# Attention over sixteen images on one core: second-pair block sums made on VectorE instead of stored and loaded, sums in fixed places, old weight form for a fourth image

## Chip, cores and metric

The kernel runs on one core of a Trainium2 chip. The metric is device time in microseconds for one launch, as the median of several runs. A second number, the time of one profiled execution, belongs to the trace that is read here.

## What is computed

The reference is a self-attention block over x of shape (16, 512, 32, 32), in float32:

```
xn = group_norm(x, 8 groups) * gamma + beta          # per image, over 64 channels x 1024 positions
q, k, v = split(qkv_w (1536 x 512) @ xn + qkv_b)     # 1x1 convolution, 4 heads of 128 channels
attn = softmax(q^T k / sqrt(128))                    # per head, 1024 x 1024
out = x + proj_w (512 x 512) @ (attn v) + proj_b
```

So each image has four heads, each with two products of 1024 x 1024 x 128, and four projections of 512 x 512 x 1024.

## The kernel before

**The main loop.** It runs over 16 images, 4 heads and 8 steps of 128 keys. A step has two halves; in each, TensorE makes a tile of scores (L1580, 128 x 512), ScalarE its exponential (L1586), and TensorE the weighted sum of the step before (L1677). VectorE adds up the exponentials for the denominators (L1601). Between these, each half-step gets a few *units* of projection work, taken from the list `halfway`. A unit is one product of a Strassen scheme, with the loads, sums and results that belong to it. Each engine's instructions stand in an order that comes from this emission and from priorities (`tc.high_priority` puts the steps that free an accumulator ahead).

**Two forms of the projections.** Images 0 to `OLD - 1` use the old form: q and k of a pair of heads, or v of all, are seven products of blocks, each again seven products, in four groups (`two_levels`, matmuls at L742, 256 columns wide). The output projection of every image has this form too. From image `OLD` on, `thirds` makes q, k and v together from x cut in three along the positions (`S3`, 342 wide): 15 products for each pair of heads, each again seven products (`strassen`, matmuls at L1168, 171 wide). These 15 are taken in eight groups (`THIRDS`) of one or two, so an image has 16 groups G: 0 to 7 for the first pair of heads, 8 to 15 for the second. A group is seven units, and a new group starts every four units. The 112 units lie in head 2 and head 3 of the image before and in head 0 of the image itself. The table `OUTER`/`FACTORS` names the seven products; the order within a group is `ORDER = (1, 2, 6, 5, 7, 4, 3)`.

**What a group needs.** First, *forms*: sums and differences of blocks of x (`FORMS_B`, made on VectorE by `make_forms`, L1043, 11 of them in six groups). Second, four inner sums t1 to t4 of the forms (`make_sum`, L1089 and L1092). Third, weights, stored earlier in DRAM as sums too (`load_weights`, on SP's queue, L1108). Both pairs of heads need the same forms and inner sums. Before, they are made for the first pair, stored to DRAM by POOL's queue (L1046 and L1095), and loaded back for the second pair by SP's queue (`load_forms` L1054, `load_sum` L1099). `HOMES` says in which of three sets of buffers a group's four sums lie, and `FOLLOWS` after which group each second-pair group may be loaded. In the function `before(k)` of `group_units`, these steps are put ahead of the k-th unit of a group: weights for the next group at k = 0 and 3, forms of the next at 1, sums of the next at 2 to 5, loads of later sums at 3 to 6, and forms to be loaded for the group after next at 3.

**Results of a group.** `out_` (L1192) adds an accumulator and an earlier copy on VectorE and so frees the accumulator; `combine` (L1256, L1265, L1278) builds q, k and v from them; `turn_v` (L982) transposes v in blocks and sends it through DRAM.

**The builder.** The weights' forms for `thirds` are made on the chip during the old-form images: `form_steps` (L1394 load, L1413 adds, L1420 stores, laid out by `BUILD_A` as head, tiles, half-steps) and then `inner_steps` for each group of the first pair (L1449 to L1452, laid out by `BUILD_B`). For the second pair, the first new-form image itself loads weights at L1429 and L1441 through `load_quads`, sums them in `sum_weights` (L1449 on) and stores them for the images after it.

Of the kernel before, what the change touches and what calls it, by code (L numbers as in the profile page):

```python
# [16 lines left out]
P = 128  # L17
# [97 lines left out]
def attention_block(  # L115
# [63 lines left out]
KC = 2  # L179
# [33 lines left out]
BUILD_B = (  # L213
    ((4, "v", (3, 10)), (5, None, (1, 8))),
    ((6, "o", (1, 8)),),
    ((8, "v", (3, 10)),),
)
FOLLOWS = {
    5: (8,), 7: (9,), 8: (10,), 9: (11,), 10: (12,), 11: (13,), 12: (14, 15),
}  # L220
# [6 lines left out]
def fast_path(ctx, tc, x, sources, out, consts, flag, dims):  # L227
# [140 lines left out]
    def halves(tiles, prefix):  # L368

        b = {  # L370
            f"b{r + 1}{h + 1}": [tiles[2 * r + k][:, ts(h, HALF)] for k in range(KC)]
            for r in range(2) for h in range(2)
        }
        b["t1"] = b["b12"]
        for n in ("t2", "t3", "t4"):
            if prefix == "x":
                t = tpool.tile([P, KC, HALF], F32, tag="f", bufs=3, name=f"x{n}")
                b[n] = [t[:, k] for k in range(KC)]
                continue
            b[n] = [  # L380
                tpool.tile([P, HALF], F32, tag=f"{prefix}{n}{k}", name=f"{prefix}{n}{k}")
                for k in range(KC)
            ]
        return b
# [269 lines left out]
    def two_levels(name, site, b, blocks, finish, sums="make", homes="BBBB", prepare=None):  # L654
# [17 lines left out]

        def sum_tile(g, m):
            k = int(m[1]) - 1
            tag = f"in_{m}" if homes[g] == "B" else f"ot{2 + k // 2}{k % 2}"
            if homes[g] == "C":
                if k % 2 == 0:
                    pairs[g] = ppool.tile([P, N], F32, tag="p", name=f"{name}_{g}_{m}")
                t = pairs[g][:, ts(k % 2, HALF)]
            else:  # L680
                t = tpool.tile([P, HALF], F32, tag=tag, name=f"{name}_{g}_{m}")
            haves[g][m] = t.rearrange("p (i q) -> p i q", q=Q)
            return haves[g][m][:, : len(OUTER[g])]

# [320 lines left out]
    def thirds(b):  # L1005
# [23 lines left out]

        def make_forms(G):  # L1030
            p, g = parts(G)
            if p or g not in FORMS_B:
                return
            n = size(G)
            forms[G] = tpool.tile([P, KC, 2, W3], F32, tag="f", bufs=3, name=f"f_{b}_{G}")

            def of(what):
                return wide_x(b, *what) if isinstance(what, tuple) else made[what]

            for i, (f, op, a, c) in enumerate(FORMS_B[g]):  # L1040
                made[f] = forms[G][:, :, i, :]
                eng = nc.vector
                (eng.tensor_add if op == "+" else eng.tensor_sub)(made[f], of(a), of(c))  # L1043
            t = dpool.tile([P, KC, n, W3], F32, tag=f"f_{g}", bufs=1, name=f"keptf_{b}_{g}")
            inner_kept[b, g, "f"] = t
            nc.gpsimd.dma_start(t, forms[G][:, :, :n, :])  # L1046

        def load_forms(G):
            p, g = parts(G)
            if p == 0 or g not in FORMS_B:  # L1050
                return
            n = size(G)
            forms[G] = tpool.tile([P, KC, 2, W3], F32, tag="f", bufs=3, name=f"f_{b}_{G}")
            nc.sync.dma_start(forms[G][:, :, :n, :], inner_kept[b, g, "f"])  # L1054

        def sum_tile(G, m):
            k = int(m[1]) - 1
            n = size(G)
            home = HOMES[G]
            tag = {"A": f"ot{2 + k // 2}{k % 2}", "B": f"in_{m}", "C": f"sg_{m}"}[home]  # L1060
            t = tpool.tile(
                [P, H3 if home == "C" else HALF], F32, tag=tag, name=f"s_{b}_{G}_{m}"
            )
            sums[G, m] = t[:, : n * H3].rearrange("p (i q) -> p i q", q=H3)
            return sums[G, m]

        def make_sum(G, m):
            p, g = parts(G)
            if p:
                return  # L1070
            n = size(G)
            to = sum_tile(G, m)
            a, c = {
                "t1": ("b12", "b11"), "t2": ("b22", "t1"), "t3": ("t2", "b11"),
                "t4": ("b21", "t2"),
            }[m]
# [16 lines left out]
            t = dpool.tile([P, n, H3], F32, tag=f"{m}_{g}_", bufs=1, name=f"kept3_{m}_{g}")  # L1093
            inner_kept[b, g, m] = t
            nc.gpsimd.dma_start(t, to)  # L1095

        def load_sum(G, m):
            g = G % count
            nc.sync.dma_start(sum_tile(G, m), inner_kept[b, g, m])  # L1099

        def load_weights(G, t):
            p, g = parts(G)
            m, n = PARTS[t], size(G)
            wts[G, t] = wpool.tile([P, 2, m, P], F32, tag=f"w{t}", name=f"w{t}_{b}_{G}")
            if first and p:
                load_quads(p, g, t, wts[G, t], nc.sync)
            else:
                nc.sync.dma_start(wts[G, t][:, :n], store3[p, g, t])  # L1108

        def sum_weights(G):  # L1110
            p, g = parts(G)
            if first and p:
# [43 lines left out]
        def group_units(G):  # L1156
# [192 lines left out]
        sizes = (2, 2) + (2, 3, 2) * 15 + (1, 2)  # L1349
        assert sum(sizes) == len(units)  # L1350
        halves_ = []
        for n in sizes:
            halves_.append(units[:n])
# [1 line left out]
        return halves_  # L1355

    store3, builder = {}, {}
    negq = one.tile([P, HEADS], F32, name="negq")
    for p_ in range(PAIRS):
        for g_, group_ in enumerate(THIRDS):  # L1360
# [116 lines left out]
    def lay_builder():  # L1477
# [9 lines left out]
        for head, where, firsts, last in BUILD_A:  # L1487
            if where:
                at(head, firsts[0], lambda where=where: take(where))
            for first in firsts:  # L1490
                for i, step in zip((0, 2, 3, 5, 6), form_steps(*chunks.pop(0))):
                    at(head, first + i, step)
            if last:
                at(head, 15, builder.clear)
        assert not chunks
        groups = [(0, g) for g in range(len(THIRDS))]
        turn = 0
        for run_ in BUILD_B:
            first = True
# [886 lines left out]
```

## Time and profile before

| | |
|---|---|
| median of 3 runs | 3219.69 us (3209.53 to 3223.44) |
| profiled execution | 3236.49 us |
| its span, first to last instruction | 3234.8 us |
| mean granted TensorE clock in it | 0.995 |

The span is that of one execution with the profiler on, 1.7 us shorter than the time of the same execution. Sums below are made against 3236.5 us and then set against the median. In the trace, x_y names with their numbers left out stand for the tiles: f is a form of x, s_t an inner sum, w weights, t_x and t_y the two accumulators, r the results, keptf and kept_t the copies in DRAM, a_o and a_v the builder's tiles.

### The profile page before, as it was taken

To read this page: it belongs to the slowest core of one execution; us is meant where nothing else is said; L and a number is where in the kernel's file an instruction comes from. 1 tells how busy PE (TensorE), PEld (TensorE's weight loads), DVE (VectorE), ACT (ScalarE), POOL (GpSimd) and SP (SyncE) were. 2 spreads that over 40 slices of the span, in tenths; PEclk is the share of its full clock that TensorE was granted. 3 is DMA by queue.
4 is the path that set the end of the run, shared out by engine and by line. 5 is a ranking of instruction groups with operands and counts; after the bars stand their busy time and mean duration, and the time that the engine had idled before them with its cause. 6 is when DMAs were issued, how large, how long until landed. Compare 5 with 4: busy or idle time off the path is not lost.

```text
span 3234.8 us, 40108 instructions
## 1 busy us (share of the span) xinstructions
PE 3143.8 (97%) x12056; PEld 2271.2 (70%) x12056; DVE 2758.0 (85%) x4959; ACT 1565.7 (48%) x3288; POOL 676.6 (21%) x1225
## 2 busy tenths in 40 slices
PE   9999999999999999999999999999999999999999
PEld 7556667677767777677777677777777767777775
DVE  9989989789698897978969789798897978979797
ACT  3534435355454554545445454454544545545443
POOL 0122122213022130321303213032131221312110
PEclk9999999999999999999999999999999999999999
DMA  5576766978869687796877967779687786877961
GB/s 172 180 233 217 250 192 197 267 244 228 253 213 280 214 240 245 224 281 207 243 234 224 273 208 235 242 225 289 207 245 248 234 265 196 262 240 236 285 194 48
DMA packets 310572, 741.67 MB, mean 229 GB/s; under 512 B 44528, under 2 KB 143616, under 8 KB 310352
## 3 DMA queue, kind: packets, MB, share of 16 engines
q1 hardware_dynamic: 200512, 410.48, 41.8%
q0 software_dynamic: 88528, 285.31, 27.6%
q10 hardware_dynamic: 21312, 43.26, 4.7%
q8 instruction: 99, 1.62, 0.2%
q14 instruction: 121, 0.99, 0.1%
HBM read 515.53 MB, written 223.35 MB: 228 GB/s over the span
## 4 chain that ended last, share of the span: by engine, by line
PE 53%; DVE 18%; DMA 12%; issue 4%; ACT 1%; POOL 1%; SPq 0%; ACTq 0%; DVEq 0%; POOLq 0%
PE s L1580 15%; PE po L1677 15%; PE t_x L1168 9%; PE t_y L1168 7%; DMA w<-kept 6%; PE pp_x L742 4%; PE pp_y L742 3%; DVE tot L1601 3%; DMA s_t<-kept_t 3%; DVE vu L982 2%; DVE r L1192 2%; DMA row<-r 1%; DVE r L1256 1%; DVE s_t L1089 1%; DVE y L1552 1%
## 5 line engine op out<-in xcount | busy, mean ns | idle before, releaser
L1580 PE MATMUL s<-qk,qk 128*128 128x512 f32 x2048 | 1051.3, 595 | 0.2 <-ACT p L1586 0.2
L1677 PE MATMUL po<-p,v 128*128 128x512 f32 x2048 | 1051.1, 595 | 0.0
L1586 ACT ACTIVATE p<-s 128x512 f32<-128x512 f32 x1024 | 610.5, 596 | 777.7 <-PE s L1580 741.6
L1677 PEld LDWEIGHTS po<-p,v 128*128 128x128 f32 x2048 | 615.8, 301 | 375.8 <-issue 258.6
L1601 DVE TENSOR_TENSOR tot<-tot,p 128x1024 f32<-128x1024 f32 (+1 forms) x408 | 471.6, 1156 | 130.2 <-ACT p L1586 128.8
L1168 PEld LDWEIGHTS t_x<-s_t,w 128*128 128x128 f32 x2340 | 397.0, 191 | 227.9 <-issue 150.0
L1168 PE MATMUL t_x<-s_t,w 128*128 128x171 f32 x2340 | 444.8, 309 | 0.8 <-DMA w<-kept 0.8
L1580 PEld LDWEIGHTS s<-qk,qk 128*128 128x128 f32 x2048 | 361.8, 190 | 37.2 <-issue 12.9
L1095 POOL DMA_DIRECT2D kept_t<-s_t x416 | 224.1, 541 | 341.8 <-DVE s_t L1089 222.7
L990 POOL DMA_DIRECT2D vd<-vu x120 | 65.8, 548 | 1089.0 <-DVE vu L982 1082.9
L1256 DVE TENSOR_TENSOR r<-r,r 128x684 f32<-128x684 f32 x286 | 243.1, 865 | 6.4 <-issue 0.2
L1192 DVE TENSOR_TENSOR r<-t_y,t_u 128x342 f32<-128x342 f32 (+1 forms) x416 | 201.3, 484 | 41.3 <-ACT t_u L1127 31.5
L1168 PE MATMUL t_y<-f,w 128*128 128x171 f32 x1144 | 203.3, 310 | 21.7 <-DVE r L1192 21.6
L1168 PEld LDWEIGHTS t_y<-f,w 128*128 128x128 f32 x1144 | 175.3, 190 | 27.7 <-DVE r L1192 27.7
L1192 DVE TENSOR_TENSOR r<-t_y,t_p 128x342 f32<-128x342 f32 x208 | 101.1, 486 | 108.1 <-ACT r L1131 94.2
L1127 ACT COPY t_u<-t_x 128x342 f32<-128x342 f32 x260 | 108.4, 417 | 167.6 <-PE t_x L1168 150.4
L742 PE MATMUL pp_x<-pp_t,w_proj 128*128 128x256 f32 x630 | 167.1, 382 | 8.2 <-ACT pp_u L613 8.2
L742 PEld LDWEIGHTS pp_x<-pp_t,w_proj 128*128 128x128 f32 x630 | 117.5, 190 | 77.2 <-issue 32.5
L1556 POOL DMA_DIRECT2D out_y<-y x120 | 65.6, 547 | 467.7 <-DVE y L1555 425.9
L995 POOL DMA_DIRECT2D v<-vd x240 | 139.6, 589 | 98.5 <-DMA vd<-vu 79.4
L1168 PE MATMUL t_y<-s_t,w 128*128 128x171 f32 x780 | 150.2, 309 | 2.9 <-DVE r L1192 1.5
L1168 PE MATMUL t_x<-f,w 128*128 128x171 f32 x572 | 114.5, 316 | 32.9 <-DMA w<-kept 32.9
(320 smaller groups left out, 4433.7 us busy)
## 6 DMA issues: line engine op xcount, KB each, us to landing
w<-kept SPq DMA_DIRECT2D x187, 512.0 KB, 5.4
w<-kept SPq DMA_DIRECT2D x187, 384.0 KB, 5.2
kept_t<-s_t POOLq DMA_DIRECT2D x364, 171.0 KB, 7.4
s_t<-kept_t SPq DMA_DIRECT2D x364, 171.0 KB, 4.9
keptf<-f POOLq DMA_DIRECT2D x65, 684.0 KB, 8.7
f<-keptf SPq DMA_DIRECT2D x65, 684.0 KB, 6.3
rinv<-row ACTq DMA_DIRECT2D x63, 512.0 KB, 5.8
x<-in_x POOLq DMA_DIRECT2D x60, 512.0 KB, 7.9
```

The lines of the kernel that those rows point to most:

```text
L742: latest["product"] = nc.tensor.matmul(acc[:, ts(i, Q)], have["w"][t][:, i, slot, :], inner(i, bn), start=(first and i == 0), stop=True, s ...
L990: nc.gpsimd.dma_start(rows[which][ts(h, P), :], u)
L995: nc.gpsimd.dma_start(vs[b, pair][ts(q, BLK), half].rearrange("m h (k i) j -> m (h k) (i j)", k=n), rows[which].rearrange("(k m) (q e) -> ...
L1095: nc.gpsimd.dma_start(t, to)
L1127: nc.scalar.copy(dst, src)
L1168: latest["product"] = nc.tensor.matmul(acc[:, ts(i, H3)], wts[G, t][:, i, slot, :], moving, start=(start and i == 0), stop=True, skip_grou ...
L1192: nc.vector.tensor_add(dst, view(a), view(c))
L1256: (nc.vector.tensor_add if add else nc.vector.tensor_sub)(at(o), a, c)
L1580: latest["score"] = nc.tensor.matmul(sc, ks[b, h][:, ts(j, P)], qs[b, h][:, ts(half, HALF)], start=True, stop=True)
L1586: exps[s] = nc.scalar.activation(ps[s][:, ts(half, HALF)], sc, AF.Exp, scale=SCALE)
L1601: added[b, h, j] = nc.vector.tensor_add(tot[b, h][:, i], tot[b, h][:, i], ps[s][:, i])
L1677: summed = nc.tensor.matmul(po[half], v_block(b, h, j), ps[s][:, i], start=(j == 0), stop=(j == NB - 1),)
```

## The change

Forms are now made on VectorE for both pairs; neither the store nor `load_forms` is left. The inner sums are still stored and loaded, but their places are three tiles that are allocated once (`home` A and B, `home_c`), and each store and load takes two sums (t1 with t2, t3 with t4). `OLD` goes from 3 to 4, so image 3 takes the old form. The builder makes inner weights for groups 0 to 5 instead of 0 to 7 (`LATE`); the first new-form image makes them for groups 6 to 15. `BUILD_A` and `BUILD_B` are laid out anew, with one run in a head, and `form_steps` leaves four half-steps between load and adds. `FLOW` has the numbers that stood in `sizes`.

```diff
-OLD = 3
-BUILD_A = ((3, "o", (0, 7), True), (7, "o", (0, 7), True))
+OLD = 4
+LATE = 6
+BUILD_A = (
+    (3, "o", (0,), True), (4, "v", (4,), True), (6, "o", (0,), False), (7, None, (0,), True),
+)
 BUILD_B = (
-    ((4, "v", (3, 10)), (5, None, (1, 8))),
-    ((6, "o", (1, 8)),),
-    ((8, "v", (3, 10)),),
+    ((8, "v", (3,)), (9, None, (2,))),
+    ((10, "o", (3,)), (11, None, (2,))),
+    ((12, "v", (3,)), (13, None, (2,))),
 )
...
+    home = {
+        h: tpool.tile([P, 4, HALF], F32, tag=f"home{h}", name=f"home_{h}") for h in "AB"
+    }
...
         def make_forms(G):
             p, g = parts(G)
-            if p or g not in FORMS_B:
+            if g not in FORMS_B:
                 return
...
-            t = dpool.tile([P, KC, n, W3], F32, tag=f"f_{g}", bufs=1, name=f"keptf_{b}_{g}")
-            inner_kept[b, g, "f"] = t
-            nc.gpsimd.dma_start(t, forms[G][:, :, :n, :])
-
-        def load_forms(G):
...
-            nc.sync.dma_start(forms[G][:, :, :n, :], inner_kept[b, g, "f"])
...
         def sum_tile(G, m):
...
+            if (G, "all") not in sums:
+                t = home_c if HOMES[G] == "C" else home[HOMES[G]].rearrange("p m q -> p (m q)")
+                sums[G, "all"] = t[:, : 4 * n * H3].rearrange("p (m i q) -> p m i q", m=4, q=H3)
+            sums[G, m] = sums[G, "all"][:, k]
...
-            nc.gpsimd.dma_start(t, to)
+            if m in ("t2", "t4"):
+                i = 2 * (m == "t4")
...
+                nc.gpsimd.dma_start(t, sums[G, "all"][:, i : i + 2])
 
         def load_sum(G, m):
             g = G % count
-            nc.sync.dma_start(sum_tile(G, m), inner_kept[b, g, m])
+            for k in range(4):
+                sum_tile(G, f"t{k + 1}")
+            i = 2 * (m == "t4")
+            nc.sync.dma_start(sums[G, "all"][:, i : i + 2], inner_kept[b, g, m])
...
-            if first and p:
+            if first and G >= LATE:
...
-                after_(G + 2, 3, load_forms)
...
-                        for kk, m in ((3, "t2"), (4, "t1"), (5, "t3"), (6, "t4")):
+                        for kk, m in ((4, "t2"), (6, "t4")):
                             after_(hh, kk, load_sum, m)
...
-                for i, step in zip((0, 2, 3, 5, 6), form_steps(*chunks.pop(0))):
+                for i, step in zip((0, 4, 5, 9, 10), form_steps(*chunks.pop(0))):
...
-        groups = [(0, g) for g in range(len(THIRDS))]
+        groups = [(0, g) for g in range(LATE)]
```

More of the change, by code (lines that the diff above doesn't have):

```diff
@@ L381, in halves @@
                 tpool.tile([P, HALF], F32, tag=f"{prefix}{n}{k}", name=f"{prefix}{n}{k}")
+                if n == "t4" else home["A"][:, 2 * (int(n[1]) - 2) + k]
                 for k in range(KC)
@@ L674, in sum_tile @@
             k = int(m[1]) - 1
-            tag = f"in_{m}" if homes[g] == "B" else f"ot{2 + k // 2}{k % 2}"
             if homes[g] == "C":
@@ L680, in sum_tile @@
             else:
-                t = tpool.tile([P, HALF], F32, tag=tag, name=f"{name}_{g}_{m}")
+                t = home[homes[g]][:, k]
             haves[g][m] = t.rearrange("p (i q) -> p i q", q=Q)
@@ L1043, in make_forms @@
                 (eng.tensor_add if op == "+" else eng.tensor_sub)(made[f], of(a), of(c))
-            t = dpool.tile([P, KC, n, W3], F32, tag=f"f_{g}", bufs=1, name=f"keptf_{b}_{g}")
-            inner_kept[b, g, "f"] = t
-            nc.gpsimd.dma_start(t, forms[G][:, :, :n, :])
-        def load_forms(G):
[L1049 to L1053, printed above, removed]
-            nc.sync.dma_start(forms[G][:, :, :n, :], inner_kept[b, g, "f"])
         def sum_tile(G, m):
@@ L1058, in sum_tile @@
             n = size(G)
[L1059 to L1064, printed above, removed]
+            if (G, "all") not in sums:
+                t = home_c if HOMES[G] == "C" else home[HOMES[G]].rearrange("p m q -> p (m q)")
+                sums[G, "all"] = t[:, : 4 * n * H3].rearrange("p (m i q) -> p m i q", m=4, q=H3)
+            sums[G, m] = sums[G, "all"][:, k]
             return sums[G, m]
@@ L1092, in make_sum @@
                         nc.vector.tensor_sub(to[:, i, :], of(a, i), of(c, i))
[L1093 to L1095 removed]
+            if m in ("t2", "t4"):
+                i = 2 * (m == "t4")
+                t = dpool.tile(
+                    [P, 2, n, H3], F32, tag=f"{m}_{g}_", bufs=1, name=f"kept3_{m}_{g}"
+                )
+                inner_kept[b, g, m] = t
+                nc.gpsimd.dma_start(t, sums[G, "all"][:, i : i + 2])
         def load_sum(G, m):
             g = G % count
[L1099 removed]
+            for k in range(4):
+                sum_tile(G, f"t{k + 1}")
+            i = 2 * (m == "t4")
+            nc.sync.dma_start(sums[G, "all"][:, i : i + 2], inner_kept[b, g, m])
         def load_weights(G, t):
@@ L1111, in sum_weights @@
             p, g = parts(G)
-            if first and p:
+            if first and G >= LATE:
                 w = [wts[G, t] for t in range(2)]
@@ L1348, in thirds @@
         )
-        sizes = (2, 2) + (2, 3, 2) * 15 + (1, 2)
-        assert sum(sizes) == len(units)
+        assert sum(FLOW) == len(units)
+        sizes = FLOW
         halves_ = []
@@ L1357, in fast_path @@
     store3, builder = {}, {}
+    home_c = tpool.tile([P, 4 * H3], F32, tag="homeC", name="home_C")
     negq = one.tile([P, HEADS], F32, name="negq")
```

1 line of the change is left out of this document (added).

## Prediction

> **What bounds the kernel now.** I began with the page, its span and its engines.
>
> ```profile
> span 3234.8 us, 40108 instructions
> PE 3143.8 (97%) x12056; PEld 2271.2 (70%) x12056; DVE 2758.0 (85%) x4959; ACT 1565.7 (48%) x3288; POOL 676.6 (21%) x1225
> ```
>
> TensorE (PE) is busy 97% of the span, so the matmuls set the time: work on another engine counts only where TensorE waits for it, and everything that a change can win lies in the 91.0 us between 3234.8 and 3143.8. VectorE (DVE) at 85% is second, and this change gives it more. The next view is the sums by stage: two heads of image 1 and the first two of image 2 (the last wholly old-form stretch), then the stretch of the first new-form image, then the twelve that follow.
>
> ```profile
> 335.90:539.60 203.70, 196.75 (x649) 137.36 (x648) 176.88 (x326) 90.41 (x168) 37.55 (x68) 1.00 0.64 210
> 539.60:749.60 210.00, 200.26 (x776) 145.83 (x776) 178.54 (x331) 100.13 (x216) 45.46 (x81) 0.97 0.82 246
> 749.60:3149.00 2399.40, 2338.68 (x9290) 1720.83 (x9289) 2038.97 (x3579) 1187.01 (x2560) 532.40 (x968) 1.00 0.78 240
> ```
>
> The columns are length, then busy time of PE, weight loads, DVE, ACT and POOL, granted clock, DMA share, GB/s. Four heads in the old form take 203.7 us, the first new-form image 210.0, a later one 2399.4 / 12 = 199.95. The waits of TensorE in the twelve-image stretch (total, times, longest):
>
> ```profile
> PE t_x L1168 <- DMA w<-kept: 33.2, 19, 4.9
> PE t_y L1168 <- DVE r L1192: 18.9, 22, 1.5
> PE pp_x L742 <- ACT pp_u L613: 6.7, 11, 0.6
> ```
>
> The largest is for weights loaded by SP: 33.2 us, 2.8 us an image. Where in an image, by head (head 2, head 3, head 0 of the next, head 1):
>
> ```profile
> 1350.60:1400.20 49.60, 49.49 (x214) 37.33 (x213) 49.33 (x92) 21.84 (x49) 18.99 (x35) 1.00 0.93 274
> 1400.20:1453.20 53.00, 49.13 (x200) 36.05 (x199) 37.04 (x61) 21.51 (x49) 10.55 (x19) 0.97 0.91 272
> 1453.20:1499.60 46.40, 46.40 (x197) 34.88 (x196) 37.30 (x58) 21.83 (x49) 0.78 (x2) 1.00 0.58 188
> 1499.60:1551.60 52.00, 50.54 (x171) 35.40 (x171) 46.25 (x91) 34.94 (x70) 14.27 (x26) 1.00 0.65 216
> ```
>
> Head 2 shows that VectorE busy 49.33 of 49.60 us costs TensorE almost nothing (49.49 busy). Head 3 loses 3.9 us, with the DMA engines 0.91 busy; head 0, at 0.58, loses nothing. The transfers of head 3 (its GB/s in 40 slices, packets in sum, then KB each and median us to landing), and at the end the same weights in head 0:
>
> ```profile
> GB/s 39 124 90 116 333 390 122 149 330 410 407 374 160 283 322 233 267 295 412 398 408 411 413 404 423 399 236 216 242 242 230 232 242 353 372 294 36 26 155 304
> DMA packets 6347, 14.43 MB, mean 272 GB/s; under 512 B 927, under 2 KB 3664, under 8 KB 6342
> f<-keptf SPq DMA_DIRECT2D x4, 684.0 KB, 7.0
> w<-kept SPq DMA_DIRECT2D x5, 512.0 KB, 9.9
> keptf<-f POOLq DMA_DIRECT2D x1, 684.0 KB, 8.9
> ...
> w<-kept SPq DMA_DIRECT2D x3, 512.0 KB, 4.2
> ```
>
> The same weights land in 9.9 us in head 3 and in 4.2 us in head 0: the waits are queueing behind other bytes.
>
> **Part 1: the forms of the second pair on VectorE.** `make_forms` no longer returns for pair 1 and no longer stores; `load_forms` is gone. Head 3 loses four loads and a store of 684 KB, 3.4 of its 14.43 MB, so at the same cost per byte its DMA share falls from 0.91 to about 0.70 (estimate from these rows), nearer to head 0's 0.58, and the weights' landing should fall towards 4.2 us. An image loses 6 issues on SP and 6 on POOL. The 33.2 us can stay whole or go whole; I keep a tenth, 0.3 us an image, because 0.70 is nearer to 0.58 than to 0.91.
>
> With the longest of these waits goes a second loss, the granted clock:
>
> ```profile
> 1041.50:1048.90 7.40, 4.58 (x12) 2.29 (x11) 1.38 (x2) 1.64 (x4) 0.00 (x0) 0.77 0.86 254
> 1441.40:1448.40 7.00, 4.11 (x10) 2.31 (x9) 1.19 (x2) 1.64 (x4) 0.00 (x0) 0.76 0.95 285
> 1642.60:1649.80 7.20, 3.92 (x10) 2.24 (x9) 1.22 (x2) 1.57 (x4) 0.00 (x0) 0.76 0.93 279
> 1843.60:1854.60 11.00, 6.13 (x15) 3.88 (x14) 1.18 (x2) 1.64 (x4) 0.00 (x0) 0.69 0.65 201
> 2050.20:2057.20 7.00, 4.07 (x21) 3.15 (x20) 1.23 (x3) 2.24 (x6) 0.00 (x0) 1.00 0.81 260
> 2646.50:2653.30 6.80, 3.93 (x10) 2.23 (x9) 1.22 (x2) 1.63 (x4) 0.00 (x0) 0.75 0.89 313
> ```
>
> Each window holds one wait. In five the clock falls; lost are at most 0.23 x 7.40 + 0.24 x 7.00 + 0.24 x 7.20 + 0.31 x 11.00 + 0.25 x 6.80 = 10.2 us, part of it inside the wait. TensorE was idle 2.9 us in the window at 2050 without losing clock, and 2.8 to 3.3 us in four of the five that lost it. I take 6 us of 0 to 10.2, a little over half. The Trainium skill, "TensorE: Matmul & The Clock Gate", section "What's actually happening", says that the clock halves only after at least one idle window of about 3.4 us. By that rule only the window at 1843 (3.4 us of the 10.2) should have lost clock, and the sum below would be some 3 to 4 us less of a gain. The rows disagree: idle times of 2.8 to 3.3 us were enough.
>
> The price is on VectorE:
>
> ```profile
> L1043 DVE TENSOR_TENSOR f<-x x52: 795/854/875, 531.7 to 3001.4; 128x684 f32<-128x684 f32 x52
> L1043 DVE TENSOR_TENSOR f<-x,f x26: 852/868/872, 567.5 to 3009.2; 128x684 f32<-128x684 f32 x26
> ```
>
> These are the first and last of four rows with 143 instructions in all, 11 for each of 13 images. Eleven more at about 0.86 us make 9.5 us an image. By the program order six fall from the end of head 2 into head 3 and the rest into head 0 and its start. Head 3 goes from 37.0 to 42.2 us of VectorE work, head 0 from 37.3 to about 41.6 in 46.4. Both stay below head 2, whose saturation TensorE did not feel. The one place without cover is this (start, us, instruction, idle before):
>
> ```profile
> 1419.00 1.06 DVE L1278 SCALAR_TENSOR_TENSOR vt<-r,vb_sb,r 128x342 f32<-128x342 f32 x2 [1.71 <-ACT r L1127]
> 1420.88 3.96 DVE L982 STREAM_TRANSPOSE vu<-vt 128x512 f32<-128x512 f32 x4
> 1424.66 1.24 DVE L1601 TENSOR_TENSOR tot<-tot,p 128x1024 f32<-128x1024 f32 x1
> 1425.79 0.53 DVE L1192 TENSOR_TENSOR r<-t_y,t_u 128x342 f32<-128x342 f32 x1
> ```
>
> Four transposes of `turn_v` and a running sum stand before the add that frees the accumulator of group 7, and TensorE waited 1.0 us for it. The forms of group 9 come before the 1.71 us of idle time, which absorbs both. One form of group 10 comes between that idle time and the add, and its second form, with those of group 11, just after it. So I add one form, 0.8 us an image, between 0 (absorbed) and 5.2 us (all six of head 3 on the path). Behind the late add are queued the next adds of group 8; only 22 waits for such adds in twelve images (about two an image) say that the others have room. That nothing of this is below nothing is plain: no VectorE instruction goes.
>
> **Part 2: fixed homes, two transfers a group.** The sums' stores go from 32 to 16 an image on POOL, their loads from 32 to 16 on SP, same bytes. The order of the waits on a piece of the home is as before; only t1 can now be overwritten when the joint store of t1 and t2 has landed, one unit later. The landing on the page:
>
> ```profile
> kept_t<-s_t POOLq DMA_DIRECT2D x364, 171.0 KB, 7.4
> ```
>
> Sixteen groups fill the 149.0 us of heads 2, 3 and 0, so a home is written anew after two groups, 18.6 us, against 7.4 us to landing. I cost this part at nothing; that distance is the cover, and if it fails, VectorE stops at `make_sum`, with all adds queued behind it. Half the issues on two queues could also be a small gain; no wait above is put down to POOL's issuing, so I count none.
>
> **Part 3: image 3 in the old form.** One image goes from 199.95 to 203.7 us as measured, but the saving above is then made in 11 images, not 12. The builder moves: one run of `form_steps` a head, with four half-steps between load and adds where there were two, and `BUILD_B` in heads 8 to 13 for six groups; so images 0 and 1 carry `form_steps`, images 2 and 3 the rest. In before, VectorE stopped for the loads of `form_steps`, and TensorE waited behind it in the old-form stretch (180.9 to 539.6 us):
>
> ```profile
>   DMA a_o<-in_qkv_wT: 13.0, 5
>   DMA kepta<-a_o: 9.3, 3
> ...
> PE qk_y L742 <- DVE qk_r L771: 5.8, 4, 2.1
> PE v_y L742 <- DVE v_r L771: 5.2, 5, 1.8
> PE v_x L742 <- ACT v_u L613: 1.7, 2, 1.2
> ```
>
> At best the 5.2 + 1.7 us of the v products go; at worst a third image adds its share of qk waits, 2.9. I take -4 (of -7 to +3).
>
> **The first new-form image** now sums weights for ten groups instead of eight, and makes its forms:
>
> ```profile
> PE t_y L1168 <- DVE r L1192: 4.5, 2, 4.1
> ...
> L1449 DVE TENSOR_TENSOR w<-w x8: 291/420/426, 616.3 to 690.1; 128x256 f32<-128x256 f32 x7, 128x128 f32<-128x128 f32 x1
> ```
>
> Four such sums a group, so at most 8 x 0.42 = 3.4 us more on VectorE, and 5.2 for the forms of head 3; against that, 3.4 MB less in its crowded head and its own lost clock (0.97 of 210 us, 6.3 us). Between -10 and +9; I take 0.
>
> **The sum.** A later image without its waits: (2399.4 - 33.2 - 6) / 12 = 196.7; with 0.3 and 0.8, 197.8. Eleven: 2175.8. With the moved image 2379.5, against 2399.4: -19.9. Builder -4: -24 against the profiled execution's 3236.5, so 3212.5, or -0.74%. The timed runs lie 16.8 us lower (median 3219.7). If they hold the same waits, after is 3196; if the whole 16.8 us are weight waits that they do not have, the gain falls to about 9 us, and after is 3211. I take the middle, **3203**.
>
> **Rivals.** *VectorE becomes the bound of head 3* (slower): the forms stand in front of the adds, and what the idle time and the slack do not take is paid eleven times. At the full 5.2 us the time is 3203 + 4.4 x 11 = 3251; it decides from 2.3 us an image, where the gain is used up. For it: the 1.0 us wait after the transposes, with nothing to spare. Against it: head 2. *The weights' waits stay*: they would come from the order on SP, where a load waits behind one that waits for TensorE, and not from bytes. Then 3.7 for the moved image, 0.8 x 11 = 9 and -4 are left: 3228. For it: the share of 0.91 moves only 272 GB/s, while eight of its slices move over 400. Against it: 9.9 against 4.2 us to landing. The Trainium skill, "Perfetto Trace Analysis", section "Roofline", puts a core's 16 DMA engines at some 435 GB/s together, by which head 3 would not be short of bytes. The trace's own busy share of 0.91 speaks against that reading. *More is gained*: the timed runs hold the same waits, and first image and builder add some 8 us: 3188. That the change leaves the loads in place is excluded by the program order: no form is loaded any more.
>
> **Chances.** Forecast 0.63, VectorE 0.10, waits stay 0.12, more 0.15. A measurement of this kernel can tell about 0.5%, 16.1 us: faster is below 3203.6, slower above 3235.8. The forecast's own span, 3192 to 3218, is split by that line, 0.35 faster and 0.28 within. Faster: 0.35 + 0.15 = 0.50; same: 0.28 + 0.12 = 0.40; slower: 0.10. The range, 3184 to 3229, takes in the waits that stay and most of the larger gain.
>
> **What would show it.** Right: weight waits under 5 us, head 3 near 50 us with a DMA share near 0.7 and clock 1.00, weights landing in 5 to 6 us there, the wait after the transposes at 1.8 us, head 0 still 46.4, VectorE busy some 110 us more. Wrong: head 3 still at 53 us with weight waits (second rival), or with waits of t_y for r over 2 us (first), a first new-form image far over 210 us, or VectorE idle at `make_sum` for a store.

## The result, and the profile after

| | before | after |
|---|---|---|
| median | 3219.49 us (4 runs, 3209.53 to 3223.44) | 3162.78 us (4 runs, 3161.16 to 3164.29) |
| ratio | | 0.9828, 95% interval 0.9806 to 0.9851 |
| profiled execution | 3236.49 us | 3161.16 us |

The kernel became 1.7% faster. The forecast had the sign right and the size wrong: 16.5 us in the timed runs where 56.7 came, 24 us in the profile where 75.3 came; 3162.8 lies below the range, 3184 to 3229. One of the ten timed runs of kernel 11 below took 6780.83 us; its ratio is made without it.

The page of after, its span, engines and transfers:

```profile
span 3159.5 us, 38471 instructions
...
PE 3123.2 (99%) x11930; PEld 2260.6 (72%) x11930; DVE 2844.3 (90%) x5081; ACT 1558.6 (49%) x3240; POOL 518.8 (16%) x935
...
DMA packets 245713, 632.69 MB, mean 200 GB/s; under 512 B 35184, under 2 KB 80368, under 8 KB 245504
```

VectorE has 86 us more to do, POOL 158 us less, and the chip moves 109 MB less than before (741.67 MB). The windows of after by stage, with the columns of before's: an image in the old form, the first new-form image, the eleven that follow, and of these one head 3:

```profile
328.40:524.40 196.00, 195.44 (x649) 137.78 (x648) 175.25 (x319) 90.85 (x168) 34.91 (x63) 1.00 0.62 205
720.40:922.60 202.20, 195.99 (x775) 143.96 (x774) 187.72 (x350) 100.04 (x216) 33.90 (x60) 0.99 0.68 223
922.60:3075.20 2152.60, 2131.02 (x8516) 1574.08 (x8516) 1951.44 (x3404) 1088.67 (x2344) 356.57 (x645) 1.00 0.65 205
...
972.20:1019.80 47.60, 47.19 (x200) 35.41 (x200) 40.83 (x66) 21.73 (x49) 8.43 (x15) 1.00 0.80 239
```

A later image takes 2152.6 / 11 = 195.7 us instead of 199.95. All of that is head 3, 47.6 us instead of 53.0 in the image shown; head 0 stays at 46.4. But an image in the old form also fell, from 203.7 to 196.0 us, and the first new-form one from 210.0 to 202.2. TensorE's waits in the eleven later images:

```profile
PE t_y L1169 <- DVE r L1193: 13.8, 23, 0.9
PE pp_x L749 <- ACT pp_u L621: 6.0, 10, 0.6
```

No wait for weights is left. The wait for r, which was to grow, shrank from 18.9 / 12 = 1.58 to 13.8 / 11 = 1.25 us an image. The weights in head 3 of after:

```profile
DMA packets 4102, 11.37 MB, mean 239 GB/s; under 512 B 628, under 2 KB 1012, under 8 KB 4100
...
w<-kept SPq DMA_DIRECT2D x5, 512.0 KB, 5.0
```

They land in 5.0 us, with the DMA engines busy 0.80 of the time instead of 0.91. That alone would fit the prediction's reason, fewer bytes. Fewer bytes are not what removes the waits, as the runs show.

### The profile page after: what moved, and what is told of

Read it like the earlier page. It is cut to its first block, busy times and chain, and to the rows that moved or that the text cites. A ratio compares the mean times of both kernels' runs of the same rounds, so it can differ in the third digit from the quotient of the medians.

```text
span 3159.5 us, 38471 instructions
## 1 busy us (share of the span) xinstructions
PE 3123.2 (99%) x11930; PEld 2260.6 (72%) x11930; DVE 2844.3 (90%) x5081; ACT 1558.6 (49%) x3240; POOL 518.8 (16%) x935
## 5 line engine op out<-in xcount | busy, mean ns | idle before, releaser
L1169 PEld LDWEIGHTS t_x<-home_B,w 128*128 128x128 f32 x1008 | 169.4, 190 | 90.7 <-issue 60.0
L1169 PEld LDWEIGHTS t_x<-home_A,w 128*128 128x128 f32 x1008 | 168.5, 190 | 88.9 <-issue 59.6
L1256 DVE TENSOR_TENSOR r<-r,r 128x684 f32<-128x684 f32 x264 | 223.9, 855 | 0.5
L1193 DVE TENSOR_TENSOR r<-t_y,t_u 128x342 f32<-128x342 f32 (+1 forms) x384 | 183.0, 477 | 14.4 <-ACT t_u L1128 9.7
L1169 PE MATMUL t_x<-home_A,w 128*128 128x171 f32 x1008 | 188.8, 309 | 0.0
L1169 PE MATMUL t_x<-home_B,w 128*128 128x171 f32 x1008 | 188.0, 308 | 0.0
L1128 ACT COPY t_u<-t_x 128x342 f32<-128x342 f32 (+1 forms) x240 | 99.9, 416 | 155.9 <-PE t_x L1169 155.9
L749 PE MATMUL pp_x<-home_B,w_proj 128*128 128x256 f32 x630 | 166.7, 381 | 6.8 <-ACT pp_u L621 6.8
L749 PEld LDWEIGHTS pp_x<-home_B,w_proj 128*128 128x128 f32 x630 | 117.9, 190 | 74.5 <-issue 32.8
L989 DVE STREAM_TRANSPOSE vu<-vt 128x512 f32<-128x512 f32 x120 | 123.4, 1100 | 0.0
```

Of the source, the lines that this page charges most:

```text
L749: latest["product"] = nc.tensor.matmul(acc[:, ts(i, Q)], have["w"][t][:, i, slot, :], inner(i, bn), start=(first and i == 0), stop=True, s ...
L989: nc.vector.transpose(u.rearrange("p (q i j) -> p j q i", q=n, i=BLK), t.rearrange("p (j q i) -> p j q i", q=n, i=BLK),)
L1128: nc.scalar.copy(dst, src)
L1169: latest["product"] = nc.tensor.matmul(acc[:, ts(i, H3)], wts[G, t][:, i, slot, :], moving, start=(start and i == 0), stop=True, skip_grou ...
L1193: nc.vector.tensor_add(dst, view(a), view(c))
L1256: (nc.vector.tensor_add if add else nc.vector.tensor_sub)(at(o), a, c)
```

## The experiments

The expectations name three theories by letter. **A** is the prediction's: weights come late because the DMA engines are busy with the forms' bytes. **B** stands in the first ones alone: most of the gain comes from the builder's layout and the fourth old image. **C** is near the prediction's second rival: weights come late because form loads stand ahead of them on SP's queue. The table gives for each kernel the time, the ratio to before on the same chip, and three lengths from its profile, cut at the starts of heads: an image of the old-form stretch after image 0 (mean), the first new-form image, a later image (mean). The last column says whether form loads stand on SP's queue. The lengths are of one execution each (kernel 2's was 12 us above the median of its runs), and kernels ran on different chips, so small differences between kernels other than before are judged by the ratios.

| kernel | us | ratio (95%) | old | first new | later | on SP |
|---|---|---|---|---|---|---|
| before | 3219 to 3225 | 1 | 203.7 | 210.0 | 199.95 | yes |
| after | 3162.78 | 0.9828 (0.9806, 0.9851) | 196.2 | 202.2 | 195.69 | no |
| 1 forms only | 3174.27 | 0.9854 (0.9823, 0.9885) | 201.2 | 204.1 | 195.71 | no |
| 2 layout only | 3210.8 | 0.9964 (0.9947, 0.9981) | 197.0 | 210.0 | 200.31 | yes |
| 3 homes only | 3189.78 | 0.9898 (0.9868, 0.9929) | 201.8 | 205.0 | 197.40 | yes |
| 4 after, forms loaded | 3189.75 | 0.9895 (0.9863, 0.9928) | 199.1 | 207.3 | 197.37 | yes |
| 5 after, forms stored twice | 3174.59 | 0.9852 (0.9821, 0.9882) | 197.7 | 211.0 | 195.65 | no |
| 6 form loads on POOL | 3183.81 | 0.9873 (0.9841, 0.9904) | 203.9 | 209.2 | 195.83 | no |
| 7 after without homes | 3166.52 | 0.9824 (0.9793, 0.9855) | 197.7 | 202.4 | 195.60 | no |
| 8 after, forms made twice | 3166.07 | 0.9825 (0.9794, 0.9857) | 196.5 | 203.7 | 195.62 | no |
| 9 homes, four transfers | 3199.33 | 0.993 (0.9907, 0.9953) | 201.5 | 202.5 | 198.04 | yes |
| 10 homes, short rows | 3224.93 | 1.0005 (0.9984, 1.0026) | 201.0 | 203.1 | 200.22 | yes |
| 11 places shifted | 3221.93 | 1.0007 (0.9987, 1.0026) | 203.0 | 200.7 | 200.00 | yes |
| 12 form steps bunched | 3172.62 | 0.9851 (0.9821, 0.9882) | 200.5 | 202.7 | 195.70 | no |
| 13 groups bunched | 3170.26 | 0.9845 (0.9815, 0.9875) | 199.1 | 202.1 | 195.67 | no |
| 14 old spacing | 3162.34 | 0.9815 (0.9785, 0.9846) | 196.0 | 199.6 | 195.66 | no |
| 15 builder for eight groups | 3163.01 | 0.9809 (0.9778, 0.9839) | 197.3 | 200.7 | 195.63 | no |

The column of later images falls into two parts: 195.6 to 195.8 us in the ten kernels whose form loads are off SP's queue, 197.4 to 200.3 in the seven where they are on it, whatever else differs.

### The three parts alone

1, before with the forms of the second pair on VectorE:

```diff
-            if p or g not in FORMS_B:
+            if g not in FORMS_B:
...
-            nc.gpsimd.dma_start(t, forms[G][:, :, :n, :])
...
-                after_(G + 2, 3, load_forms)
```

> The kernel before with one part of the change: the forms of the second pair are made on VectorE, neither stored nor loaded. Theory A (the gain comes from the bytes of the forms: the weight waits of head 3 and the clock lost in them go in every new-form image): about 35 us under before, near 3184 us, no wait of t_x for w over 1 us, later images near 196 us. Theory B (most of the gain comes from the new layout of the builder and the fourth old image): at most 15 us under before, 3205 us or more, old-form stretch unchanged in both theories at about 203 us for four heads.

2, before with `OLD = 4`, `LATE = 6`, the new `BUILD_A` and `BUILD_B` and the new spacing of `form_steps`:

> The kernel before with the other part alone: OLD = 4, LATE = 6, the new BUILD_A and BUILD_B and four half-steps between load and adds of form_steps. Theory A: old-form images fall from 203.7 to about 196 us because VectorE no longer stops for the builder's loads, so some 15 to 20 us are gained: 3200 us; the weight waits of later images stay at about 2.8 us an image. Theory B: 40 us or more, 3180 us. The forecast on record would have it at 3219 (3.7 for the moved image, -4 for the builder).

3, before with the fixed places and two transfers a group, as in the change's `sum_tile`, `make_sum` and `load_sum`:

> The kernel before with fixed places and two transfers a group alone; forms are still stored and loaded. Theory A, as on record: nothing, within 5 us of 3219.5. Rival (half the issues and waits on SP let the weights start earlier): 10 to 20 us less, 3200 to 3210, with weight waits of 1 to 2 us an image instead of 2.8.

The forms alone bring later images to their floor. The layout alone brings old-form images near theirs, 197.0, and leaves the later ones with their waits. The homes alone take over half of the later images' loss. Alone the parts are worth 1.5%, 0.4% and 1.0%, together 1.7%: homes and forms work on the same loss. B is refuted by kernels 1 and 2. Three of these expectations missed in time: kernel 1 came at 3174 where 3184 was named, kernel 2 at 3211 where 3200 was, and kernel 3 at 3190, below both of its ranges, though its waits for weights (16.1 us in all) are those of the second.

### Bytes, or order on SP's queue

4, after with the forms stored and loaded as before:

```diff
+            if p or g not in FORMS_B:
...
+            nc.sync.dma_start(forms[G][:, :, :n, :], inner_kept[b, g, "f"])
```

> The kernel after with the forms of the second pair stored and loaded as before. Theory A: it loses what the forms brought, about 35 us, near 3198, weight waits of 2 to 3 us an image back. Theory B: it loses 15 us or less, 3178 or under. If the parts add up, its distance to before is that of the layout alone and the homes alone together.

5, after with the forms of both pairs stored by POOL and never loaded, so that as many bytes move as in kernel 4:

```diff
                 (eng.tensor_add if op == "+" else eng.tensor_sub)(made[f], of(a), of(c))
+            t = dpool.tile([P, KC, n, W3], F32, tag=f"f_{g}", bufs=1, name=f"keptf_{b}_{g}")
+            inner_kept[b, g, "f"] = t
+            nc.gpsimd.dma_start(t, forms[G][:, :, :n, :])
```

> The kernel after, with the forms of both pairs also stored to DRAM by POOL's queue and never loaded: as many form transfers and bytes as before, none of them on SP's queue and none that SP waits for. If the bytes on the DMA engines were what made the weights late (theory A), the weight waits come back: 20 to 35 us over after, 3183 to 3198. If what counted was the loads in SP's order, each a wait ahead of the weights (theory C), it stays within 8 us of after, under 3171.

6, before with one word changed, so that the same loads stand on POOL's queue:

```diff
-            nc.sync.dma_start(forms[G][:, :, :n, :], inner_kept[b, g, "f"])
+            nc.gpsimd.dma_start(forms[G][:, :, :n, :], inner_kept[b, g, "f"])
```

> The kernel before with one edit: the second pair's forms are still stored and loaded, with the same bytes and at the same places of the program, but their loads are issued by POOL's queue instead of SP's. Theory C (a form load standing on SP's queue ahead of the weights delays them): the weight waits of TensorE, 33 us in before, fall below 6 us, and the time comes near 3180, as in the kernel that only makes the forms on VectorE (3174), though 741 MB are moved as before. Theory A (the bytes on the DMA engines): the weight waits stay near 33 us and the time near 3220. A third outcome: POOL's own stores are held up by the loads in front of them, the waits for r or for sums grow, and the time is above 3220 although the weight waits are gone.

Kernels 4 and 5 move the same bytes, 725.17 and 725.18 MB: with loads on SP TensorE waits 12.0 us for weights, with stores on POOL not at all.

```profile
PE t_x L1180 <- DMA w<-kept: 12.0, 7, 3.2
```

The times of both lie between the ranges that were named. Kernel 4 is 27 us over after. Kernel 5 is 11.8 us over it, where C allowed 8; in its profile that lies in the first new-form image (211.0 against 202.2) and the old-form ones, and nothing of it in the later images.

Kernel 6 is the sharpest in time. Its twelve later images and one head 3 (1387.7 us on), then the transfers of that head:

```profile
749.00:3099.00 2350.00, 2324.76 (x9290) 1717.11 (x9289) 2038.83 (x3579) 1186.46 (x2560) 574.92 (x1040) 1.00 0.79 245
...
1387.70:1435.70 48.00, 47.20 (x200) 35.42 (x200) 36.77 (x60) 21.56 (x49) 12.79 (x23) 1.00 0.98 295
```

```profile
DMA packets 6257, 14.16 MB, mean 295 GB/s; under 512 B 913, under 2 KB 3644, under 8 KB 6255
...
f<-keptf POOLq DMA_DIRECT2D x4, 684.0 KB, 8.5
w<-kept SPq DMA_DIRECT2D x5, 512.0 KB, 7.9
```

The DMA engines are busy 0.98 of this head, more than before's 0.91, with the same 14 MB, and the head takes 48.0 us. Weights still need 7.9 us to land. In the twelve later images TensorE waits 1.2 us for weights instead of 33.2:

```profile
PE t_y L1168 <- DVE r L1192: 15.5, 22, 1.1
PE pp_x L742 <- ACT pp_u L613: 6.6, 11, 0.6
PE t_x L1168 <- DMA w<-kept: 1.2, 3, 0.6
```

What was late can be seen at one load. SP's issues in before, ahead of the 2.9 us wait at 1444.5 us, and then what the load issued at 1430.9 met:

```profile
1427.25 0.32 SPq L1108 DMA_DIRECT2D w<-kept  x1
1427.66 0.45 SPq L1054 DMA_DIRECT2D f<-keptf  x1
1429.55 0.90 SPq L1099 DMA_DIRECT2D s_t<-kept_t  x2
1430.93 0.32 SPq L1108 DMA_DIRECT2D w<-kept  x1
```

```profile
L1108 SPq DMA_DIRECT2D w<-kept x1: 320/320/320, 1430.9 to 1430.9; - x1
...
  PE t_x L1168: 2.9, 1
...
DMA to landing us min/median/max: 13.5/13.5/13.5
```

These weights, 30.7 us into the head, had the form load of 684 KB and two sums in front of them on the queue. Counted from the issue of the weights, the form landed after 6.9 us, the sums after 9.4 and 11.9, and the weights themselves after 13.5, at 1444.4. TensorE had been ready for 2.9 us, so it needed them 10.6 us after their issue. The same load in kernel 6, 30.1 us into its head:

```profile
L1108 SPq DMA_DIRECT2D w<-kept x1: 422/422/422, 1417.8 to 1417.8; - x1
...
DMA to landing us min/median/max: 6.3/6.3/6.3
```

It lands in 6.3 us. The form load comes later now: on POOL's queue it follows the eight transfers of v and is issued at 1424.9, 37.2 us into the head instead of 27.5.

```profile
1417.73 4.65 POOL L995 DMA_DIRECT2D v<-vd  x8 [4.75 <-issue]
1424.91 0.58 POOL L1054 DMA_DIRECT2D f<-keptf  x1 [2.53 <-PE s L1580]
```

So the bytes alone don't make TensorE wait, and A is refuted as the cause of the waits. With C there is a limit: kernel 6 changes the queue and, with it, the moment of the load. In none of its twelve later images is a form load under way when this load of weights is issued. Kernel 5's trace parts the two further. Its same load, 30.0 us into a head 3 that starts at 1376.6, and the two form stores of 684 KB that POOL issues just behind it:

```profile
L1112 SPq DMA_DIRECT2D w<-kept x1: 423/423/423, 1406.6 to 1406.6; - x1
...
DMA to landing us min/median/max: 7.9/7.9/7.9
```

```profile
L1053 POOL DMA_DIRECT2D keptf<-f x2: 554/564/574, 1409.3 to 1409.8; - x2
...
DMA to landing us min/median/max: 8.2/9.2/10.2
```

With these stores beside it on another queue, the load lands in 7.9 us. In the traces of all eleven later images of kernel 5 it has such stores beside it and takes 7.0 to 9.5 us; in the twelve of before it stands behind a form load on SP's queue each time and takes 10.0 to 15.3 us. That speaks for the queue. It isn't a full proof: these are stores and not loads, and kernel 5 also has fewer loads of sums on SP's queue.

Weights do land later while forms are loaded, from either queue. Over all weight loads of the twelve later images, those issued while a form load was under way landed after a median of 9.1 us in before (98 loads, the longest 15.3) and of 8.0 us in kernel 6 (100 loads, the longest 10.8); with none under way it was 5.0 and 4.9 us. Part of this difference can come from the stretches in which form loads stand, which are crowded with other transfers too. Against the 10.6 us above, a landing like kernel 6's costs TensorE next to nothing, and one like before's 13.5 costs a wait.

The Trainium skill, "DMA: Bandwidth & Descriptors", section "Issuing engines are not separate DMA queues", says that all queues end on the same 16 DMA engines, and that issuing from several saves only the sequencer's small issue time. The 8.0 us against 4.9 fit shared engines. That only issue time is saved does not: the one word was worth 3224.7 - 3183.8 = 41 us, since it decided which load lands when.

### Is VectorE near its limit?

8, after with each form of the second pair made twice (the same results):

```diff
+                if p:
+                    (eng.tensor_add if op == "+" else eng.tensor_sub)(made[f], of(a), of(c))
```

> The kernel after with each form of the second pair made twice on VectorE (11 more instructions of some 0.86 us an image, 9.5 us, same results). It prices the rival of VectorE as the bound, whose point was a wait after the transposes. If the idle time of VectorE in heads 3 and 0 takes them as it took the first set: within 5 us of after, 3158 to 3168. If after already stands at the edge: a large part is paid in 12 images, 20 to 110 us, 3183 to 3270, and the waits of t_y for r grow from 1.2 us an image to over 3.

```profile
PE 3125.9 (99%) x11930; PEld 2260.9 (71%) x11930; DVE 2940.4 (93%) x5213; ACT 1556.9 (49%) x3240; POOL 519.0 (16%) x935
```

96 us more on VectorE cost 3166.1 - 3162.8 = 3 us at most (by the ratios, 0.9825 and 0.9828, nothing), and none in the later images (195.62). The first rival is far from its point.

### What the homes are worth

7, after without the fixed places and joint transfers (kernels 1 and 2 in one):

> The kernel after without the fixed places and the joint transfers: forms on VectorE and the new layout (image 3 old, new builder) on the kernel before. If the homes gain only by fewer issues on SP ahead of the weights, nothing of it is left once the form loads are gone: within 6 us of after, 3157 to 3169. If the placing or the packets gain by themselves, as the kernel with four transfers in fixed places (3199 against 3222) hints, it is 15 to 30 us slower than after, 3178 to 3193. Steady later images then show it: 195.7 us an image in the first case, above 197 in the second.

The ratios, 0.9824 and 0.9828, are the same within their intervals of 0.003. Once no form load stands on SP's queue, the homes bring nothing that can be measured.

9, kernel 3 with four transfers a group; 10, kernel 3 with the two sums of a transfer apart in DRAM, so that its runs are as short as before:

```diff
-                    [P, 2, n, H3], F32, tag=f"{m}_{g}_", bufs=1, name=f"kept3_{m}_{g}"
+                    [2, P, n, H3], F32, tag=f"{m}_{g}_", bufs=1, name=f"kept3_{m}_{g}"
```

> The kernel before with the fixed places alone, four transfers a group as before. The homes alone with two transfers gave 3190. If the fixed places did it, this is also near 3190. If the halved number of transfers did it, this is near before, 3215 to 3225, with weight waits of about 2.8 us an image.

> The kernel before with fixed places and two transfers a group, but the two sums lie apart in DRAM, so that every transfer is cut into runs of 1368 bytes as before and not 2736. If the number of issues and waits on SP counts (theory C), it is near the homes alone, 3190. If the length of the runs counts (fewer packets for the same bytes), it is near before, 3215 or more.

11, before with a small tile allocated ahead of all others:

```diff
+    pad = one.tile([P, 128], F32, name="pad")
+    nc.gpsimd.memset(pad, 0.0)
```

> The kernel before with one unused tile of 512 bytes a partition allocated ahead of the others (cleared once by POOL), so that the buffers behind it lie elsewhere and nothing else changes. If the gain of the fixed places with four transfers (3199 against 3222) came from where the buffers lie, or from a queue on SP that is so close to its limit that any small shift moves it, this kernel too is off by 8 us or more in either direction: outside 3214 to 3230. If the order or the waits of the transfers made that gain, this one stays at 3217 to 3227.

Kernel 10 halves the issues and gains nothing, so the number of issues is not what the homes gain by. From kernel 3 it differs only in the length of its runs in DRAM, and lies 35 us above it. The transfers of kernel 3 and then of kernel 10, the same bytes in fewer and in more packets:

```profile
DMA packets 271044, 741.57 MB, mean 232 GB/s; under 512 B 37872, under 2 KB 86208, under 8 KB 270832
...
DMA packets 303492, 741.57 MB, mean 230 GB/s; under 512 B 37872, under 2 KB 139040, under 8 KB 303280
```

So where two sums go in one transfer, the longer runs make the gain, as the expectation for kernel 10 had it for this outcome. But kernel 9 gains 0.7% with short runs and as many issues as before, between both of its ranges. Kernel 11 shows that this other placing is worth nothing by itself. Why fixed places with four short transfers gain, as long as the form loads are there, stays open.

### The builder's layout

12, after with `BUILD_A` and the spacing of before; 13, after with the groups two in a head; 14, after with the old spacing alone; 15, after with `LATE = 8`:

```diff
# 12
+BUILD_A = ((3, "o", (0, 7), True), (7, "o", (0, 7), True))
# 12 and 14
+                for i, step in zip((0, 2, 3, 5, 6), form_steps(*chunks.pop(0))):
# 13
+    ((8, "v", (3, 10)), (9, None, (1, 8))),
+    ((10, "o", (3, 10)),),
# 15
+    ((10, "o", (3,)), (11, None, (2, 9))),
+    ((12, "v", (3,)), (13, None, (2, 9))),
```

> The kernel after with the builder's form steps bunched as before: two pieces in head 3 and two in head 7, with the earlier distance of two half-steps between load and adds; the inner weights stay in heads 8 to 13. If the spreading of the form steps is what made the old-form stretch cheaper (13.9 us lost over the steady pace of heads 3 to 10 before, 4.3 after by the layout), most of that comes back: 5 to 12 us over after, 3168 to 3175, with waits of the products for v's results again. If it is the spreading of the inner weights, nothing comes back: 3160 to 3165.

> The kernel after with the six inner-weight groups of the builder bunched two in a head, in heads 8, 9 and 10, instead of one in a head from 8 to 13; the form steps stay spread. If bunched sums of weights on VectorE hold up the products of the old-form images, 3 to 10 us come back: 3166 to 3173. If only the form steps mattered: 3160 to 3165.

> The kernel after with two half-steps between load and adds of form_steps, as before. If VectorE's stops for the builder's loads cost the old-form images their time, it loses 5 to 10 us against after (3168 to 3173), in heads 3, 4, 6 and 7 of the program. If it was the spreading of BUILD_A and BUILD_B over more heads, it loses under 3 us.

> The kernel after with the builder making inner weights for eight groups of the first pair (LATE 8 and two more places in heads 11 and 13), so that the first new-form image makes them for eight groups instead of ten. If the first new-form image loses time (202.2 us against 195.7 for a later one) to the sums of weights on VectorE, a quarter to a half of its 6.5 us goes and the old-form images keep theirs: 3159 to 3162, a gain of 1 to 4 us over after. If VectorE in the old-form images has no room for two groups more, they take back 2 to 6 us: 3163 to 3169.

Bunching costs 9.8 us in kernel 12 and 7.5 in 13 by the medians; by the ratios it is some 7 and 5 us, and the intervals overlap after's. The profiles agree with the medians: three old-form images are 13 us longer in kernel 12 and 9 in 13. The spacing costs nothing (3162.34 against 3162.78). Kernel 12's waits in its old-form stretch, TensorE's and then VectorE's, show the way it takes:

```profile
PE qk_y L749 <- DVE qk_r L778: 6.8, 2, 4.6
PE v_y L749 <- DVE v_r L778: 3.2, 4, 1.0
```

```profile
DVE a_o L1414 <- DMA a_o<-in_qkv_wT: 10.0, 4, 4.4
DVE a_v L1450 <- DMA a_o<-kepta: 8.9, 2, 5.5
```

VectorE stops for the builder's transfers, and what frees TensorE's accumulators stands behind it. VectorE's waits for `in_qkv_wT` there are 0.5 us in after, and those of L1450 for `kepta` 3.1. VectorE's longest stop and TensorE's longest wait stand one behind the other in head 8, with the add between them that frees the accumulator:

```profile
465.74 0.43 DVE L1450 TENSOR_TENSOR a_v<-a_o 128x256 f32<-128x256 f32 x1 [5.47 <-DMA a_o<-kepta]
...
471.96 0.68 DVE L778 TENSOR_TENSOR qk_r<-qk_y,qk_u 128x512 f32<-128x512 f32 x1
...
472.70 1.65 PE L749 MATMUL qk_y<-xt,w 128*128 128x256 f32 x3 [4.55 <-DVE qk_r L778]
```

Kernel 13 has one wait of 4.3 us, of a product of the output projection, in head 9, in which two groups are made. Kernel 15 moves the work of two groups out of the first new-form image (200.7) into the old-form ones (197.3) and is no faster. None of these beats after by more than the noise.

## Why the prediction was wrong, step by step

The direction was right, and the waits for weights went as forecast. The steps that failed are the builder's term, -4 in the sum where the trace shows 720.4 - (539.6 + 203.7) = -22.9 us, the length of a later image, 197.8 where 195.7 came, and the reason given for the waits. By the prediction's own stretches, in the profiled executions:

| stretch | forecast | measured | missed |
|---|---|---|---|
| up to the first new-form image | 539.6 + 203.7 - 4 = 739.3 | 720.4 | -18.9 |
| first new-form image | 210.0 | 202.2 | -7.8 |
| eleven later images | 2175.8 | 2152.6 | -23.2 |
| the end | 85.8 | 84.3 | -1.5 |

**Part 1, the reason.** The waits went, as forecast, but "queueing behind other bytes" was a failed step as far as it means bytes wherever they are queued. The row with 9.9 and 4.2 us allowed two readings, and the DMA share of 0.91 was taken for a limit; kernel 6 runs at 0.98 with 1.2 us of such waits in twelve images. That the waits went as forecast in spite of this reason was luck: the change takes away the forms' bytes and their place on SP's queue together. The second rival was right that the order on SP counts, and wrong in its way and its outcome. The load that came late was not held up before its issue (30.7 us into the head, 30.1 in kernel 6), as a load behind one that waits for TensorE would be; it spent its 13.5 us after it. And waits from the order on SP go too when the change takes the loads off that queue.

**Part 1, the size.** 23.2 / 11 = 2.1 us an image. The 0.3 kept for weights was 0. The 0.8 for VectorE was 0. VectorE at the transposes of the head 3 that starts at 972.2:

```profile
990.77 0.85 DVE L1050 TENSOR_TENSOR f<-x,x 128x684 f32<-128x684 f32 x1
991.55 0.85 DVE L1256 TENSOR_TENSOR r<-r,r 128x684 f32<-128x684 f32 x1
992.33 2.99 DVE L989 STREAM_TRANSPOSE vu<-vt 128x512 f32<-128x512 f32 x3
995.18 1.20 DVE L1602 TENSOR_TENSOR tot<-tot,p 128x1024 f32<-128x1024 f32 x1
996.31 1.08 DVE L989 STREAM_TRANSPOSE vu<-vt 128x512 f32<-128x512 f32 x1
997.24 0.48 DVE L1193 TENSOR_TENSOR r<-t_y,t_u 128x342 f32<-128x342 f32 x1
```

There is no idle time in it: the 1.71 us that the prediction saw took the form, as its "0 (absorbed)" had it. The last row is the add that frees group 7's accumulator; it comes 25.0 us into the head, where it came 25.6 us in (1425.79 - 1400.2) before. The rest, 1.0, is the clean image, 195.7 instead of 196.7. If the clock loss was all of its bound, 10.2 instead of 6, that is 0.35; the smaller wait for r is 0.33; some 0.3 are not traced.

**Part 2** was costed at nothing, and that held here (kernel 7). It was not nothing where the form loads stay (kernel 3).

**Part 3** failed most. The moved image was put at +3.7 and the builder at -4, of -7 to +3. The old form was taken to be dearer by itself, but 203.7 held the builder's stops: spread out, an image of old form takes 196.0, against 195.7 of the new. The failed step is the bound "at best the 5.2 + 1.7 us of the v products": it held the waits of qk, 5.8 us, to be there in any case, and even a third image to add to them. In the old-form stretch of after, one image longer, they are 2.1 us and those of v are gone:

```profile
PE qk_y L749 <- DVE qk_r L778: 2.1, 2, 1.2
```

**The first new-form image** was put at 0 of -10 to +9 and came at -7.8. This doesn't bear much: kernel 11, before in all but its places, has 200.7 us there at a clock of 1.00, where before had 210.0 at 0.97. One profile of this image is not to be trusted to better than some 9 us.

**From profile to timed runs.** 16.8 us between before's profile and its median were halved. After's profile (3161.16) lies 1.6 us below its median (3162.78). So 75.3 - 56.7 = 18.6 us of the gain in the profile is not in the timed runs: the halving took too little off. Which losses of before's profiled execution these were isn't shown.

**VectorE as the bound** was refuted by kernel 8. Of what was to be seen, the waits for weights under 5 us, the clock and head 0's 46.4 came true, as did weights landing in 5 to 6 us in head 3; head 3 came at 47.6 us, not near 50, the DMA share at 0.80, not 0.7, VectorE's work rose by 86 us, not 110, and the waits for r, of which the one after the transposes was to grow to 1.8 us, are 0.9 us at the longest.

## What to carry to other kernels

When a load is late, look first at what its own queue issued ahead of it and whether that was needed as soon; a high busy share of the DMA engines is no proof that bytes are the limit. Moving the same load to another queue is a test of one word, but it can move the load in time too, so the trace has to be read for both. A stretch that looks dear because of the form of its work may be dear because of other work laid into it; find out what VectorE waits for there before the form is priced. Where several parts of a change act on the same loss, their worth alone doesn't add up.

## What was not expected of the hardware

TensorE's clock was halved after shorter waits than in before. In kernel 3, a wait of 1.88 us, and the window around it (granted clock 0.76):

```profile
2413.57 0.91 PE L1176 MATMUL t_x<-f,w 128*128 128x171 f32 x3 [1.88 <-DMA w<-kept]
```

```profile
2411.00:2418.00 7.00, 5.12 (x16) 3.08 (x15) 1.67 (x2) 1.64 (x4) 0.00 (x0) 0.76 0.74 243
```

The rule of 3.4 us of idle time that the prediction quoted from the Trainium skill, "TensorE: Matmul & The Clock Gate", section "What's actually happening", did not hold here either. And a head 3 at 295 GB/s and a DMA share of 0.98 (kernel 6) took 48.0 us, against after's 47.6 at 0.80, so that a share near 1.00 was no sign of a stall.
